# Gated cross-attention and mixture of experts on one core: another way to turn two batches, another gate layout, and a written order for loads and list fills

## The chip, the core and the metric

The kernel runs on one core of a Trainium2 chip. The metric is device time in microseconds (us) for one execution; the time of a kernel is the median of its runs. A core has five engines that run their own instruction streams and meet at semaphores: TensorE (PE; its weight loads are listed as PEld), VectorE (DVE), ScalarE (ACT), GpSimd (POOL) and SyncE (SP), which here mainly issues DMAs. Everything is computed in float32. Matrix products go to PSUM, a small memory from which DVE or ACT must copy the result before the buffer can be used again.

## The reference, cut to what matters

Four batches of 512 rows, 512 columns. Each batch goes through a cross-attention with 64 context rows and 16 heads, then through a mixture of 8 experts with the best 2 per row, plus one shared expert:

```python
x = x + tanh(g_xattn[0]) * xattn(layernorm(x), ctx, Wq, Wkv_expand, Wout)
x = x + tanh(g_ffn[0]) * ffn(layernorm(x), gate_w, w1, w2, w3, ws1, ws2, ws3)
...
# xattn: q = xn @ Wq.T; scores = q k / sqrt(32), causal mask, softmax, @ v, @ Wout.T
# ffn:
scores = softmax(xf @ gate_w.T)                 # 2048 x 8
weights, idx = top_k(scores, 2)
g = silu(xf @ w1[e].T) * (xf @ w3[e].T)
y = sum over the chosen e of weight * (g @ w2[e].T)
z = silu(xf @ ws1.T) * (xf @ ws3.T) @ ws2.T      # shared expert
```

## The kernel before, in words

**Tiling.** A batch is four token tiles of 128 rows (`QT = 4`), and 512 columns are four chunks of 128 (`DC = 4`). A product over 512 columns needs its input turned, columns on the partitions. Two normalised forms of every batch are turned: the first rows (input of the query projection, tile `xt`) and the second rows (input of the feed-forward part, tiles `x2t`). `turn` (L500) does it on PE: four 128x128 transposes for each token tile go to one PSUM buffer, and ACT copies that to SBUF (`transpose_rows`, L194).

**Attention loop (L693 to L795).** It runs over b = 0 to 3. In turn b PE does the scores of batch b, the first turn of batch b+1 (`turn(xn, xt)`, L701), the output projection of batch b-1 (`project_out`, L367, one 512-wide product for each token tile, product `pd`), the other half of the scores, the query projection of batch b+1 in four chunks (`project_q`, product `pq`), the turning of the probabilities (`transpose_p`, L340, product `pp`), the second turn and the gate of batch b-1, and the attention product (`po`). DVE meanwhile does masks, maxima, differences and sums of the softmax in four parts p0 to p3 (`largest`, `exponentials`, `softmax`), adds the projection to x (L374), takes moments (L156) and normalises (L185). ACT does exponentials and copies PSUM to SBUF. POOL divides by the sums (L338).

The order on PE, POOL, DVE and ACT is the order of the program text (`manual_schedule`, L844); what SP issues was placed by a scheduler. The four PSUM buffers of the pool `ps_mm` go round in order of allocation, so a product waits until the buffer of the fourth one before it has been copied out.

**Gate (L378 to L396).** `gate` does, for each of four column chunks k, one product of 32 gate columns (8 of them used) with all 512 tokens, each into its own 32 partitions of one buffer. ACT copies the 128x512 result; `gate_sum` then adds the four parts with four products, whose stationary operand is a 128x128 block of the parts and whose moving operand is `part`, a 0/1 matrix of 128x8. The result, tokens on partitions, goes to `choose` (L408), which finds the two best experts, the weights and the running counts.

**Routing.** `route` (L451) makes each row's place in a list per expert in DRAM (`xg_d`); POOL writes the rows there with indirect DMAs (L474). After the last batch, `fill_ends` (L535) writes a tile of null rows behind each of the eight lists: for each a register is loaded from SBUF and a DMA issued, all on SP. `tile_table` (L545) makes the table of tiles.

**Expert stage (from L998).** PE goes through the tiles of the lists: `hidden` (L911), `turn_g`, `down` (L939). A tile's rows come by SP's DMAs (`fetch`, L876) and are turned by DVE (`turn`, L900, in 32x32 blocks: the rows were stored with their columns permuted, `normalize(..., turned=True)`, and the DMA puts every fourth part on its own 32 partitions). POOL adds the results to `y_d` by indirect DMA (L949). Between attention and experts PE does products of the shared expert (`shared_in_turn`, L629), placed between the steps of the last routing by `fill`. At the end the sums are read back, added and stored.

**Loads.** Shared-expert weights `sh13` use the memory of `wq_sb`, so their load (L599) waits for the last query projection. `w13_all` (L850) and `w2_all` (L857) are loaded for all experts, 1 MB and 0.5 MB each; `w2_all` needs memory that the pool `al` (weights `wo_sb` and the attention output `at`) gives back.

Of the kernel before, what the change touches and what calls it, by code (L numbers as in the profile page):

```python
# [13 lines left out]
F32 = mybir.dt.float32  # L14
I32 = mybir.dt.int32
AF = mybir.ActivationFunctionType
ALU = mybir.AluOpType
AX = mybir.AxisListType

P = 128  # L20
B, S, D = 4, 512, 512
SK, L = 64, 128
NH, HD = 16, 32
NE, FF = 8, 256
DC = D // P
QT = S // P
NT = B * QT
FC = FF // P
# [8 lines left out]
ROWS = NE * REGION + (MAXT - TOPK * B * S // P) * P  # L37
# [11 lines left out]
def gated_cross_attention_moe(  # L49
# [14 lines left out]
    nc = tc.nc  # L64
    const = ctx.enter_context(tc.tile_pool(name="const", bufs=1))
    small = ctx.enter_context(tc.tile_pool(name="small", bufs=2))
    ET = mybir.EngineType
# [29 lines left out]
    y_d = dram.tile([2 * (B * S + P), YH], F32, name="y_d")  # L97
    y_rows = y_d.rearrange("(r h) d -> r (h d)", h=2)
    xg_w = dram_disjoint_views(xg_d, TOPK * NT + NE)
    y_w = dram_disjoint_views(y_d, 2)  # L100

    ident = const.tile([P, P], F32, name="ident")
    make_identity(nc, ident)
    ones = const.tile([P, P], F32, name="ones")
    nc.gpsimd.memset(ones, 1.0)

    part = const.tile([P, NE], F32, name="part")
    nc.gpsimd.tensor_copy(part, ident[:, 0:NE])
    for c in range(1, DC):
        nc.gpsimd.tensor_tensor(part, part, ident[:, c * HD : c * HD + NE], ALU.add)  # L110

    before = const.tile([P, P], F32, name="before")
    nc.gpsimd.affine_select(
# [40 lines left out]
    def moments(b, mv, t):  # L154
        st = small.tile([P, 6], F32, tag="st", name="st")
        nc.vector.bn_stats(st, xs[b][:, t, :])  # L156
        nc.vector.bn_aggr(mv[:, t, :], st)
# [21 lines left out]
    def normalize(xn, b, t, mv, rstd, turned=False):  # L179

        src = xs[b][:, t, :]
        if turned:
            src = src.rearrange("p (c a i) -> p a c i", c=DC, a=DC)
            xn = xn.rearrange("p (a c i) -> p a c i", a=DC, c=DC)
        nc.vector.tensor_scalar(  # L185
            xn, src, mv[:, t, 0:1], rstd[:, t, :], ALU.subtract, ALU.mult
        )

    def second_rows(w, c):


        return w[:, c, :].rearrange("(a i) n -> i a n", a=DC)
# [15 lines left out]
    x2t = [rows_sb[:, 0 : DC * S].rearrange("p (c s) -> p c s", c=DC)] + x2t  # L208

    ending = ctx.enter_context(ExitStack())  # L210
    al = ending.enter_context(tc.tile_pool(name="al", bufs=1, side="right"))
    weights = ctx.enter_context(ExitStack())

    with ExitStack() as attn:
# [162 lines left out]

        def gate(b):  # L378

            pg = ps_mm.tile([P, S], F32, tag="mm", name="pg")  # L380
            for k in range(DC):
                nc.tensor.matmul(
                    pg[k * HD : (k + 1) * HD, :], gate_sb[:, k, :], x2t[b][:, k, :],
                    start=True, stop=True,
                )
            parts = xr.tile([P, S], F32, tag="gate", name="parts")
            nc.scalar.copy(parts, pg)
            return parts

        def gate_sum(parts):  # L390
            pl = ps_mm.tile([P, QT, NE], F32, tag="mm", name="pl")
            for t in range(QT):
                nc.tensor.matmul(
                    pl[:, t, :], parts[:, ts(t, P)], part, start=True, stop=True
                )
            return pl  # L396

        full = [P, QT, NE]

# [92 lines left out]

        def first_rows(b, rest):
            rest()
            xn = [a4.tile([P, D], F32, tag="xn", name="xn") for t in range(QT)]
            for t in range(QT):
                normalize(xn[t], b, t, mv1[b], rstd1[b])
            return xn

        def turn(xn, dst):  # L500
            for t in range(QT):
                transpose_rows(xn[t], t, dst)
# [32 lines left out]
        def fill_ends(n):  # L535

            end = const.tile([P, NE], I32, name="end")
            nc.vector.tensor_tensor(end, n[:, :, 0], region[:, 0, :], ALU.add)
            for e in range(NE):
                r = nc.sync.value_load(end[0:1, e : e + 1], min_val=0, max_val=ROWS - P)  # L540
                nc.sync.dma_start(
                    out=xg_w[TOPK * NT + e][ds(r, P), :], in_=zeros[:, 0, :]
                )

# [51 lines left out]


        sh13 = const.tile([P, 2, DC, FF], F32, tag="wq_sh", name="sh13")
        for c in range(DC):  # L599
            for w in range(2):  # L600
                nc.sync.dma_start(
                    out=sh13[ts(c, HD), w], in_=second_rows(w13[0, :, w], c)
                )

        def shared_half(b, f, w, ph=None):
            if ph is None:
# [35 lines left out]


        def attention():
            xn = [a4.tile([P, D], F32, tag="xn", name="xn") for t in range(QT)]
            nc.gpsimd.tensor_copy(ctx_sb[:, :, 1, :], ctx_sb[:, :, 0, :])
            small_one = small.tile([P, 1], F32, tag="one", name="one", bufs=1)

# [44 lines left out]
            for b in range(B):  # L693
# [4 lines left out]
                    places, scatter = route(last - 1, *chosen)  # L698
                if more:
                    xt, qt_next = new_xt(), new_qt()  # L700
                    turn(xn, xt)  # L701
                if not b:
                    project_values(1)
                p0 = exponentials(*largest(psc, 0))
# [15 lines left out]
                if b:  # L720
                    for t in range(1, QT):
                        project_out(last, at, t)
                        moments(last, mv, t)
                    rest = deviation(mv, rstd)
                    if more:
                        table_of(AF.Exp)
                else:
                    project_q(xt, qt_next, range(2))
                    first_rest = first_moments(b + 2)
                    table_of(AF.Exp)  # L730
# [26 lines left out]
                if b:  # L757
                    transpose_p(p0, prt, 0)
                    transpose_p(p1, prt, 1)
                    turn(xn2, x2t[last])  # L760
                if more:
                    project_q(xt, qt_next, range(2, 3))
                    if b + 2 < B:
                        if b:
                            first_rest = first_moments(b + 2)
                            table_of(AF.Exp)
                        xn = first_rows(b + 2, first_rest)
                    project_q(xt, qt_next, range(3, DC))
                    if b:
                        scored = gate(last)  # L770
                else:
                    p3 = exponentials(*p3)
                    softmax(p3)
                    gated, scored = shared_pair(*next(parts), lambda: gate(last))
                    gated()
                    scores = gate_sum(scored)
                transpose_p(p2, prt, 2)
                if not b:
                    project_values(2)
                elif more:  # L780
                    scores = gate_sum(scored)
                transpose_p(p3, prt, 3)
                if not b:
                    project_values(3)
# [18 lines left out]
        def last_routing(at, chosen, parts):  # L803
            ps_f = ending.enter_context(tc.tile_pool(name="ps_f", bufs=2, space=PSUM))
            filling = shared_in_turn(parts, ps_f)

            def fill(n):
                for _ in range(n):
                    next(filling)

            def scatter_all(places, scatter):
                places()
                for t in range(QT):
                    scatter(t)

            b = B - 1
            xn2 = addressed([rows_sb[:, ts(t, ROW)] for t in range(QT)], b)
            mv, rstd = new_stats()
            for t in range(QT):
                project_out(b, at, t)  # L820
                if not t:
                    scatter_all(*route(b - 1, *chosen))
                moments(b, mv, t)
            deviation(mv, rstd)()
            second_rows_of(xn2, b, mv, rstd)
            fill(5)
            turn(xn2, x2t[b])
            fill(1)
            scored = gate(b)
            fill(1)  # L830
            chosen = choose(b, gate_sum(scored))
            fill(6)
            places, scatter = route(b, xn2, *chosen)
            n = counted()
            places()
            fill_ends(n)
            for t in range(QT):
                scatter(t)
            table = tile_table(n)
            for _ in filling:  # L840
                pass
            return table

        with tc.manual_schedule(engines={ET.PE, ET.Pool, ET.DVE, ET.Activation}):  # L844
            attended_last = attention()

            wup = weights.enter_context(tc.tile_pool(name="wup", bufs=1, reuse_waits="tile"))
            w13_all = wup.tile([P, NE, 2, DC, FF], F32, name="w13_all")
            for e in range(NE):
                nc.sync.dma_start(out=w13_all[:, e], in_=w13[1 + e])  # L850
            row_of, expert_of, rank_of, more = last_routing(*attended_last)

    ending.close()
    wdn = weights.enter_context(tc.tile_pool(name="wdn", bufs=1, reuse_waits="tile"))
    w2_all = wdn.tile([P, NE, FC, D], F32, name="w2_all")
    for e in range(NE):
        nc.sync.dma_start(out=w2_all[:, e], in_=w2[1 + e])  # L857

    turned.close()
    fp = ctx.enter_context(tc.tile_pool(name="fp", bufs=6, side="right", reuse_waits="tile"))  # L860
    tp = ctx.enter_context(tc.tile_pool(name="tp", bufs=3, side="right", reuse_waits="tile"))
# [259 lines left out]
```

## Time and profile before

| | us |
|---|---|
| median of 3 runs | 466.2 (465.54 to 466.81) |
| the profiled execution | 468.26 |
| its span, first to last instruction | 466.5 |
| attention, from the first scores to the last attention product | about 28 to 188 |
| last routing and shared expert | about 188 to 244 |
| expert tiles | about 244 to 433 |
| sums read back and stored | about 433 to 466 |

The granted TensorE clock was 0.998. Busy time, by stretches of the span:

| stretch, us | PE | DVE | ACT | POOL |
|---|---|---|---|---|
| 58.00 to 75.20 | 17.20 | 13.31 | 6.33 | 4.73 |
| 75.20 to 87.60 | 12.40 | 11.73 | 7.56 | 1.20 |
| 100.50 to 118.70 | 18.20 | 16.23 | 6.96 | 4.95 |
| 118.70 to 131.20 | 12.50 | 11.80 | 7.63 | 9.90 |
| 258.00 to 433.00 | 174.53 | 65.48 | 24.26 | 101.75 |

A row of the chain of waits is: start, length, engine, product and line. A row of the timeline is: start, length, engine, line, operation, output and inputs, shapes, count, and in brackets how long the engine was idle before it and what released it. Matmuls in float32 appear as two records each, transposes as one.

### The profile page before, as it was taken

How to read it: one execution, taken by the hardware profiler on the slowest of the kernel's cores; microseconds unless marked ns; L12 is line 12 of the kernel's file. 1: busy time of each engine (PE TensorE's matmuls, PEld its weight loads, DVE VectorE, ACT ScalarE, POOL GpSimd, SP SyncE). 2: the span in 40 equal slices, each digit the busy share in tenths (PEclk: the TensorE clock that was granted, in tenths of full speed). 3: DMA queues.
4: the chain of work that ended last, by engine and by line, in shares of the span. 5: the costliest groups of instructions: out<-in, count | busy, mean ns of one | idle time of the engine just before them, and what ended most of it. 6: DMA issues, size and time to landing. Idle time of an engine off the chain costs nothing.

```text
span 466.5 us, 6220 instructions
## 1 busy us (share of the span) xinstructions
PE 452.7 (97%) x1718; PEld 233.2 (50%) x1718; DVE 253.2 (54%) x605; ACT 131.2 (28%) x245; POOL 178.7 (38%) x188
## 2 busy tenths in 40 slices
PE   8999999999999989999999999999999999999894
PEld 6775455664555554445444444444444444444342
DVE  4659788779927984557322443333443333432385
ACT  2347652773454265413011111111111111111000
POOL 3003312302740473241500555555565655565300
PEclk9999999999999999999999999999999999999999
DMA  8996000000413040899883777666656666544498
GB/s 264 320 332 229 0 1 0 1 1 1 160 39 80 15 170 2 313 415 379 333 245 85 150 130 118 101 107 99 100 90 96 97 112 99 79 48 48 56 382 331
DMA packets 55423, 65.66 MB, mean 141 GB/s; under 512 B 11728, under 2 KB 40144, under 8 KB 54224
## 3 DMA queue, kind: packets, MB, share of 16 engines
q1 hardware_dynamic: 42736, 47.57, 32.4%
q0 software_dynamic: 12352, 17.57, 20.9%
q8 instruction: 17, 0.28, 0.3%
q14 instruction: 30, 0.25, 0.2%
q10 hardware_dynamic: 288, 0.00, 0.0%
HBM read 34.84 MB, written 30.27 MB: 140 GB/s over the span
## 4 chain that ended last, share of the span: by engine, by line
PE 84%; DMA 7%; DVE 6%; ACT 1%; issue 1%; SPq 0%; DVEq 0%
PE ph L915 24%; PE pd L370 12%; PE py L942 11%; PE pq L292 11%; PE ph L635 6%; DMA y_d<-y,meta 5%; PE ph L609 5%; PE psc L306 3%; PE pt L198 3%; PE pp L345 2%; DVE yk L1046 2%; PE po L359 2%; PE early L609 1%; PE pg L934 1%; DVE yk L1065 1%; DMA yk<-y_d 1%
## 5 line engine op out<-in xcount | busy, mean ns | idle before, releaser
L949 POOL DMA_INDIRECT y_d<-y,meta x68 | 105.6, 1553 | 103.4 <-DVE y L946 58.4
L915 PE MATMUL ph<-w_all,xgt 128*128 x272 | 122.5, 593 | 0.1
L338 POOL TENSOR_TENSOR pr<-pr,rs 128x1024 f32<-128x1024 f32 x16 | 30.3, 1901 | 117.7 <-DVE rs L337 103.5
L915 PEld LDWEIGHTS ph<-w_all,xgt 128*128 128x128 f32 x272 | 49.0, 190 | 49.8 <-issue 49.7
L942 PE MATMUL py<-w_all,gt 128*128 x136 | 63.9, 592 | 0.0
L926 DVE SCALAR_TENSOR_TENSOR g<-sl,w,ph 128x256 f32<-128x256 f32 x34 | 16.3, 480 | 83.8 <-ACT sl L924 81.3
L292 PE MATMUL pq<-xt,wq_sb 128*128 128x512 f32 (+1 forms) x160 | 56.9, 511 | 1.6 <-ACT prt L348 0.9
L370 PE MATMUL pd<-wo_sb,at 128*128 128x512 f32 x128 | 56.1, 595 | 0.0
L924 ACT ACTIVATE sl<-ph 128x256 f32<-128x256 f32 x34 | 13.1, 385 | 109.0 <-PE ph L915 61.1
L292 PEld LDWEIGHTS pq<-xt,wq_sb 128*128 128x128 f32 x160 | 29.7, 190 | 25.5 <-issue 20.1
L942 PEld LDWEIGHTS py<-w_all,gt 128*128 128x128 f32 x136 | 25.8, 190 | 32.5 <-issue 32.5
L946 DVE COPY y<-py 128x512 f32<-128x512 f32 x34 | 23.5, 692 | 27.8 <-PE py L942 27.8
L370 PEld LDWEIGHTS pd<-wo_sb,at 128*128 128x128 f32 x128 | 23.9, 190 | 29.1 <-issue 27.5
L976 PE MATMUL pz<-sh,gs_sb 128*128 128x512 f32 (+1 forms) x68 | 28.1, 570 | 1.7 <-DVE y L946 1.2
L635 PE MATMUL ph<-x2t,sh 128*128 128x512 f32 x64 | 28.6, 597 | 0.0
L936 ACT COPY gt<-pg 128x256 f32<-128x256 f32 x34 | 12.7, 373 | 53.1 <-PE pg L934 53.1
L903 DVE STREAM_TRANSPOSE xgt<-xg 128x512 f32<-128x512 f32 x34 | 23.9, 703 | 3.0 <-DMA xg<-xg_d 3.0
L156 DVE BATCH_NORM_STATS2 st<-x 128x6 f32<-128x512 f32 x32 | 21.7, 679 | 5.0 <-DMA x<-in_x_dram 4.5
L976 PEld LDWEIGHTS pz<-sh,gs_sb 128*128 128x128 f32 x68 | 12.7, 190 | 16.8 <-issue 15.4
L330 ACT ACTIVATE pr<-pr 128x1024 f32<-128x1024 f32 x16 | 17.0, 1064 | 13.6 <-DVE pr L329 10.9
L335 DVE TENSOR_REDUCE sm<-pr 128x16 f32<-128x1024 f32 x16 | 19.1, 1194 | 2.2 <-ACT pr L330 2.2
L329 DVE TENSOR_TENSOR pr<-psc,mx 128x1024 f32<-128x1024 f32 x16 | 19.5, 1219 | 0.4
(168 smaller groups left out, 495.7 us busy)
## 6 DMA issues: line engine op xcount, KB each, us to landing
xg<-xg_d SPq DMA_DIRECT2D x144, 64.0 KB
w_all<-in_w_dram SPq DMA_DIRECT2D x8, 1024.0 KB
y_d<-gs_sb SPq DMA_DIRECT2D x1, 4352.0 KB
w_all<-in_w_dram SPq DMA_DIRECT2D x8, 512.0 KB
yk<-y_d SPq DMA_DIRECT2D x8, 512.0 KB
out_dram<-yk SPq DMA_DIRECT2D x15, 256.0 KB
x<-in_x_dram SPq DMA_DIRECT2D x3, 1024.0 KB
xg_d<-gs_sb SPq DMA_DIRECT2D x8, 264.0 KB
```

Source lines behind the costliest of these rows:

```text
L156: nc.vector.bn_stats(st, xs[b][:, t, :])
L292: nc.tensor.matmul(pq, wq_sb[:, k, ts(c, P)], xt[:, k, tokens], start=(k == 0), stop=(k == DC - 1),)
L338: nc.gpsimd.tensor_tensor(pr, pr, rs.broadcast_to([P, NH, SK]), ALU.mult)
L370: nc.tensor.matmul(pd, at[:, c, ts(t, P)], wo_sb[:, c, :], start=(c == 0), stop=(c == DC - 1),)
L609: nc.tensor.matmul(ph, sh13[:, w, k, ts(f, P)], x2t[b][:, k, :], start=(k == 0), stop=(k == DC - 1),)
L635: nc.tensor.matmul(ph[:, w, :], sh13[:, w, k, ts(f, P)], x2t[b][:, k, :], start=(k == 0), stop=(k == DC - 1),)
L903: nc.vector.transpose(xgt.rearrange("p c t k -> p t c k"), xg.rearrange("p t (c i) -> p t c i", c=DC))
L915: nc.tensor.matmul(ph, xgt[:, k, :], w13_all[:, ds(e, 1), :, k, :], start=(k == 0), stop=(k == DC - 1),)
L942: nc.tensor.matmul(py, gt[:, f, :], w2_all[:, ds(e, 1), f, :], start=(f == 0), stop=(f == FC - 1))
L946: nc.vector.tensor_copy(y, py)
L949: nc.gpsimd.indirect_dma_start(out=y_w[h], out_offset=IndirectOffsetOnAxis(ap=goes[j][:, h : h + 1].bitcast(I32), axis=0), in_=y[:, ts(h, ...
L976: nc.tensor.matmul(pz, gs[b][:, f, ts(t, P)], sh2[:, f, columns], start=(f == 0), stop=(f == FC - 1),)
```

## The change

Six things change.

1. The first rows of batches 2 and 3 are no longer turned on PE. Once normalised (with permuted columns) they are written to DRAM by four DMAs on SP and read back by four more, each to 32 partitions; DVE then turns them with four instructions (`turn_blocks`), placed after the second token tile's moments in turns b = 1 and 2. `turn(xn, xt)` stays for batch 1 alone (b = 0). The rows of a batch are one tile now, with one buffer that the rows read back share.
2. In turns 1 and 2 the second turn (`turn(xn2, x2t[last])`) comes after the third chunk of the query projection, not before it.
3. The gate puts a token tile, not a column chunk, in each group of 32 partitions: 16 products of 32 columns with 128 tokens, the four chunks added in PSUM. ACT copies 128x128, and one PE transpose takes the place of `gate_sum`. `part` and the four POOL instructions that made it are gone.
4. `fill_ends` issues every other list's register load and DMA on ACT's queue.
5. SP joins the engines in written order. The `sh13` load is written after batch 3's query projection.
6. The pool `al` is closed after the last output projection, and all eight `w2_all` loads are written there, ahead of `fill_ends`.

```diff
+    xn_d = {b: dram.tile([S, D], F32, name=f"xn_d{b}") for b in range(2, B)}
...
-    part = const.tile([P, NE], F32, name="part")
-    nc.gpsimd.tensor_copy(part, ident[:, 0:NE])
-    for c in range(1, DC):
-        nc.gpsimd.tensor_tensor(part, part, ident[:, c * HD : c * HD + NE], ALU.add)
...
-            pg = ps_mm.tile([P, S], F32, tag="mm", name="pg")
+            pg = ps_mm.tile([P, P], F32, tag="mm", name="pg")
             for k in range(DC):
-                nc.tensor.matmul(
-                    pg[k * HD : (k + 1) * HD, :], gate_sb[:, k, :], x2t[b][:, k, :],
-                    start=True, stop=True,
-                )
-            parts = xr.tile([P, S], F32, tag="gate", name="parts")
-            nc.scalar.copy(parts, pg)
-            return parts
-
-        def gate_sum(parts):
-            pl = ps_mm.tile([P, QT, NE], F32, tag="mm", name="pl")
-            for t in range(QT):
-                nc.tensor.matmul(
-                    pl[:, t, :], parts[:, ts(t, P)], part, start=True, stop=True
-                )
-            return pl
+                for t in range(QT):
+                    nc.tensor.matmul(
+                        pg[ts(t, HD), :], gate_sb[:, k, :], x2t[b][:, k, ts(t, P)],
+                        start=(k == 0), stop=(k == DC - 1),
+                    )
+            scores = xr.tile([P, P], F32, tag="gate", name="scores")
+            nc.scalar.copy(scores, pg)
+            return scores
+
+        def by_token(scores):
+            pl = ps_mm.tile([P, QT, HD], F32, tag="mm", name="pl")
+            nc.tensor.transpose(pl.rearrange("p t e -> p (t e)"), scores, ident)
+            return pl[:, :, 0:NE]
...
         def first_rows(b, rest):
             rest()
-            xn = [a4.tile([P, D], F32, tag="xn", name="xn") for t in range(QT)]
+            xn = new_xn()
             for t in range(QT):
-                normalize(xn[t], b, t, mv1[b], rstd1[b])
-            return xn
+                normalize(xn[t], b, t, mv1[b], rstd1[b], turned=b > 1)
+            return passed(xn, b) if b > 1 else xn
+
+        def new_xn():
+            xn = ab.tile([P, QT, D], F32, tag="xn", name="xn")
+            return [xn[:, t, :] for t in range(QT)]
+
+        def passed(xn, b):
+            for t in range(QT):
+                nc.sync.dma_start(out=xn_d[b][ts(t, P), :], in_=xn[t])
+            xg = ab.tile([P, QT, QT, P], F32, tag="xn", name="xg")
+            for a in range(DC):
+                nc.sync.dma_start(
+                    out=xg[ts(a, HD)].rearrange("k t tb n -> k (t tb) n"),
+                    in_=xn_d[b][:, ts(a, P)].rearrange("(t k) n -> k t n", k=HD),
+                )
+            return xg
+
+        def turn_blocks(xg, dst):
+            for t in range(QT):
+                nc.vector.transpose(
+                    dst[:, :, ts(t, P)].rearrange("p c (tb k) -> p tb c k", k=HD),
+                    xg[:, t].rearrange("p tb (c i) -> p tb c i", c=DC),
+                )
...
-                r = nc.sync.value_load(end[0:1, e : e + 1], min_val=0, max_val=ROWS - P)
-                nc.sync.dma_start(
+                queue = nc.scalar if e % 2 else nc.sync
+                r = queue.value_load(end[0:1, e : e + 1], min_val=0, max_val=ROWS - P)
+                queue.dma_start(
...
-                    turn(xn, xt)
+                    if not b:
+                        turn(xn, xt)
...
                     for t in range(1, QT):
                         project_out(last, at, t)
                         moments(last, mv, t)
+                        if more and t == 1:
+                            turn_blocks(xn, xt)
...
                     transpose_p(p1, prt, 1)
-                    turn(xn2, x2t[last])
+                    if not more:
+                        turn(xn2, x2t[last])
                 if more:
                     project_q(xt, qt_next, range(2, 3))
+                    if b:
+                        turn(xn2, x2t[last])
...
                     project_q(xt, qt_next, range(3, DC))
+                    if b == B - 2:
+                        load_shared()
...
+            outputs.close()
+            wdn = weights.enter_context(tc.tile_pool(name="wdn", bufs=1, reuse_waits="tile"))
+            w2_all = wdn.tile([P, NE, FC, D], F32, name="w2_all")
+            for e in range(NE):
+                nc.sync.dma_start(out=w2_all[:, e], in_=w2[1 + e])
             deviation(mv, rstd)()
...
-        with tc.manual_schedule(engines={ET.PE, ET.Pool, ET.DVE, ET.Activation}):
+        with tc.manual_schedule(engines={ET.PE, ET.Pool, ET.DVE, ET.Activation, ET.SP}):
...
-    wdn = weights.enter_context(tc.tile_pool(name="wdn", bufs=1, reuse_waits="tile"))
-    w2_all = wdn.tile([P, NE, FC, D], F32, name="w2_all")
-    for e in range(NE):
-        nc.sync.dma_start(out=w2_all[:, e], in_=w2[1 + e])
```

## The prediction, made before the changed kernel was run

> **What bounds the kernel now.** I read the page first, then the chain of waits, then the timelines of DVE and ACT around the stage that the turns are taken from. On the page the reader is to see that PE is nearly all of the span, and what one DVE transpose costs, in a place where its rows have also come back from DRAM.
>
> ```profile
> PE 452.7 (97%) x1718; PEld 233.2 (50%) x1718; DVE 253.2 (54%) x605; ACT 131.2 (28%) x245; POOL 178.7 (38%) x188
> L903 DVE STREAM_TRANSPOSE xgt<-xg 128x512 f32<-128x512 f32 x34 | 23.9, 703 | 3.0 <-DMA xg<-xg_d 3.0
> ```
>
> From 185.77 to 432.5 us PE has no gap worth naming, and the tail behind its last tile hangs on that tile. So what PE gains or loses up to about 185 us the end gains or loses, if nothing new stalls behind it. The chain of waits (start, length, engine, product, line) in turn b = 1 shows what PE does there:
>
> ```profile
> 59.62 1.90 PE pt L198 x16
> 61.52 13.73 PE pd L370 x32
> 75.25 1.99 PE psc L306 x32
> 77.24 7.06 PE pq L292 x16
> 84.30 1.75 PE pp L345 x16
> 86.05 1.75 PE pt L198 x16
> 87.80 6.87 PE pq L292 x16
> 94.67 1.00 PE pg L382 x8
> 95.66 1.02 PE pp L345 x8
> 96.69 0.79 PE pl L393 x8
> 97.48 0.50 PE pp L345 x4
> ...
> 98.01 0.60 ACT prt L348
> ```
>
> The change removes the `pt` row at 59.62 (and its twin of 1.80 us in b = 2), shortens `pl`, and splits `pg`. All of it stands on the chain; the question is what else is nearly as late. DVE's timeline (the bracket is its idle time and the releaser) shows the spare time in which the new transposes must lie, first b = 1, then b = 2:
>
> ```profile
> 71.86 0.75 DVE L374 SCALAR_TENSOR_TENSOR x<-pd,tg_x,x 128x512 f32<-128x512 f32 x1
> 75.29 0.75 DVE L374 SCALAR_TENSOR_TENSOR x<-pd,tg_x,x 128x512 f32<-128x512 f32 x1 [1.74 <-PE pd L370]
> 77.29 1.23 DVE L324 TENSOR_REDUCE mx<-psc 128x16 f32<-128x1024 f32 x1
> 81.69 1.22 DVE L329 TENSOR_TENSOR pr<-psc,mx 128x1024 f32<-128x1024 f32 x1
> ...
> 116.63 0.72 DVE L374 SCALAR_TENSOR_TENSOR x<-pd,tg_x,x 128x512 f32<-128x512 f32 x1
> 118.82 0.75 DVE L374 SCALAR_TENSOR_TENSOR x<-pd,tg_x,x 128x512 f32<-128x512 f32 x1 [0.52 <-PE pd L370]
> ```
>
> ACT's timeline shows that behind DVE's last score difference (81.69) ACT has only 0.56 and 0.27 us free before the copies on which PE's third query chunk depends:
>
> ```profile
> 83.01 1.06 ACT L330 ACTIVATE pr<-pr 128x1024 f32<-128x1024 f32 x1 [0.56 <-DVE pr L329]
> 84.34 0.59 ACT L296 COPY qt<-pq 128x512 f32<-128x512 f32 x1 [0.27 <-PE pq L292]
> 84.83 1.57 ACT L348 COPY prt<-pp 128x512 f32<-128x512 f32 x3
> ```
>
> **The turns.** At face value PE loses 1.90 + 1.80 = 3.70 us (ACT loses eight copies too). DVE gains four transposes per turn. One after another, large DVE instructions there follow at about 0.09 us less than their length, so I take 0.62 us a step, 2.47 us in all (bound above: 4 x 0.703 = 2.81). They stand ahead of the third token tile's residual, where the row 71.86 is. In b = 1, PE's `pd` tiles come 1.90 us earlier, but DVE reaches the third tile at 71.86 + 2.47 = 74.33, the fourth at 75.9 (steps of 1.52 to 1.58 us, from the same instructions in b = 3), and the score maximum at 77.63 instead of 77.29: the idle 1.74 us has been eaten and 0.34 more. The last score difference then ends at 83.25, ACT's exponential starts at 83.35, its copy of query chunk 1 at 84.32 (0.97 us a step) and the first copy of turned weights runs 84.81 to 85.40. PE would have ended query chunk 1 at 82.40, but the last group of `pp` needs that chunk copied, and chunk 2 takes the PSUM buffer that the first `pp` copy frees (a ring of four): it starts at about 85.45. From there chunk 2, the second turn and chunk 3 are 3.43 + 1.75 + 3.43 = 8.61, so the gate starts at 94.06 where it stood at 94.67. Of the 1.90 us only 0.61 arrives. In b = 2 DVE had only 0.52 us free, so the same sum is worse: entering 1.19 us early (0.61 and the first gate), DVE reaches the score maximum 0.46 us later than before and the gate starts only 0.34 us earlier. PE came in 1.19 early; so this turn loses 0.85. Both turns together: -0.61 + 0.85 = +0.24 us, that is, nothing of the 3.70. Bounds: -3.70 if ACT and DVE do not hold PE, +0.9 with the longer step in both turns.
>
> **Rows by way of DRAM.** Batch 2's rows are normalised by 55.38 and wanted at 71.9: 16.5 us for 1 MB out and 1 MB back. Fast bound: the peak slice of 415 GB/s, 2 x 2.5 us. Slow bound: the last store of expert rows to its use took 5.46 us, and loads of rows in the expert stage at 92 GB/s would take 11.4: 16.9 together, 0.4 us late. Nearly nothing else moves there (0 to 1 GB/s in the page's slices) and SP's queue is idle, so I take 0. Batch 3's rows have 96.3 to 115.5: more. SP's later `sh13` loads stand behind a wait for a query chunk either way: 0. What would cost: landing after 71.9, since the waiting transpose holds the residuals behind it, and they hold `x`, the maxima and so ACT's exponentials.
>
> **The second turn**, moved behind chunk 2, is the same work: 0. Chunk 2 (3.43 us) now covers the normalising of its rows. `part`'s four POOL instructions (0.18 to 0.19 us) lay ahead of a wait for a DMA: 0.
>
> **The gate.** Per batch, `pl` goes from eight records (0.79) to one transpose, 0.11 by the `pp` rows (1.75 / 16): -0.68. `pg` goes from 8 records of 512 columns to 32 of 128, still over four column groups. Lower bound: eight records per group at 107 ns (a `pq` record of 512 columns takes 430 ns, a quarter is 107), 0.86. Upper bound: `psc`, also 32 records of 128 columns but only two row groups wide, 1.99. `psc` keeps each group busy 124 ns a record, eight of which are 0.99; with starting I take 1.1, nearest to the row of today's gate, 1.00, whose streamed columns per group are the same. Net -0.68 + 0.10 = -0.58 per batch, -2.32 for four; ACT's copy is 128 wide rather than 512, cheaper, and the wait for the weight copy at 98.01 stays as short. In b = 3 PE waited 1.37 us at 172.16 for such a copy; I leave that as it is. Each tenth in the gate's length is 0.4 us in the sum; the break-even lies at 1.62.
>
> Against that stands one more row and one rule. The weight loads of `po` start 16 within 0.18 us, so the sequencer is not slow there. The Trainium skill, "TensorE: Matmul & The Clock Gate", section "Back-to-back issue gap", says that with hardware decoding off each small matmul costs about 62 ns to issue; 32 of them would be 1.98 us (an estimate from that page), and the sum +1.4 instead of -2.1. No row here shows such a limit by itself. Another rule speaks against moving the turn: "VectorE: DVE Perf Modes", section "Rules for kernel authors", sends a 128x128 transpose to TensorE. The rows agree in price, 109 ns a block on PE against 703 / 4 = 176 on DVE; it is whose time is scarce that decides.
>
> **The expert stage.** `fill_ends` took SP 12.29 us for eight fills, 1.54 each. Four on ACT hold its queue about 6.1 us from 219.25 to 225.4, or to 228.7 if ACT's register load is as much slower as its row elsewhere (0.68 against 0.44 us). Behind them wait ACT's silu (0.60) and DVE's product (0.69) of the shared part, whose PSUM buffer PE wants at 227.25: 225.4 gives 226.7, in time; 228.7 gives 230.0, 2.8 us late. I take 0, by SP's row of the same instruction. The `w2` loads all going out ahead frees the first expert gather from traffic, and it is needed sooner: the first transposed rows were ready 0.34 us before PE wanted them. I take 0, with up to 1.7 us lost if the gather is no earlier.
>
> **Sum.** 0.24 - 2.32 = -2.1 us, against the profiled 468.26 (span 466.5 and 1.8 around it). The three times had a median of 466.2; the difference is applied to that: 464.1. About 1.4 us, 0.3%, is what a measurement of this kernel tells from no change.
>
> **The rivals.**
> 1. The turns come off whole: PE is held by nothing, -3.70 - 2.32 = -6.0, 460.2. For: DVE is 54% busy and waits for `pd`. Against: the 0.27 us of ACT above. Chance 0.09.
> 2. The small products of the gate do not overlap as today's do. At `psc`'s 1.99 the gate costs 4 x (0.99 - 0.68) = +1.24, and with 0.24 the sum is +1.5: 467.7, slower; one after another (32 x 107 ns = 3.4) +7. It decides from 1.62 us on. For: `psc`. Against: `psc` has two groups, the gate four. Chance 0.16.
> 3. The rows come back late. Each microsecond after 71.9 is one on DVE, so on PE; 2.5 late in each turn gives +2.9, 469.1. It decides from about 1.1 us in each. For: the read back takes pieces of 128 elements, 512 bytes, in a rearranged order. Against: idle DMA engines. Chance 0.10.
> 4. ACT's fills hold the silu: up to +2.8, 464 to 467. Chance 0.07.
>
> **How the numbers follow.** The forecast has 0.58: mostly faster (0.43), some same (0.13), as a gate of 1.3 would bring it within 1.4 us of before. With rival 1 and a part of 4, faster is 0.54; same 0.20; slower 0.26. The range runs from 461.3 (half the turns' gain) to 468.2 (gate at `psc`'s rate, and some lateness); outside are rival 1 whole, a serial gate and rows more than 2 us late, under 2 in 10. The forecast's own range is 463 to 465.5.
>
> **What would show it.** PE waits in b = 1 and 2 ahead of query chunk 2, ended by ACT's `prt` or `qt` copy; four DVE transposes of 0.70 with no idle time by a DMA; `pg` at 1.0 to 1.2 us and `pl` at 0.11; no PE wait for ACT's L640 silu or for `xgt`; the tail as long as before. It is wrong if `pg` is near 2, if the transposes wait for `xg`, or if PE's `pd` to `pq` run without a gap.

## The result and the profile after

| | us |
|---|---|
| before, median of 20 runs | 466.16 (465.17 to 467.89) |
| changed, median of 20 runs | 465.13 (463.39 to 466.65) |
| ratio | 0.9974, 95% interval 0.9961 to 0.9986 |
| profiled run of the changed kernel | 463.80 (span 462.1), clock 0.998 |

The change gains a quarter of a per cent where 2.1 us, 0.45%, was forecast; two later comparisons (experiment 5) find less, 0.5 and 0.3 us, and can't tell that from nothing. The profiled run stands 4.5 us under that of before (468.26), which no pair of medians shows: 2.9 us of it belong to the first profile of before alone, as experiment 1 shows.

The chain of waits of the changed kernel in turn b = 1 (start, length, engine, product, line):

```profile
56.12 2.01 PE psc L304 x32
58.16 1.24 DVE psc L321
...
70.27 2.49 DVE xt L517 x4
73.43 0.70 DVE st L153
76.20 1.28 ACT L162
78.71 1.14 DVE pr L327
79.84 1.14 DVE mx L322
81.01 1.24 DVE pr L327
82.39 0.90 issue
84.57 3.53 PE pq L290 x8
88.10 1.75 PE pt L195 x16
89.85 3.44 PE pq L290 x8
93.28 1.01 PE pg L382 x32
```

Before, this stretch was PE's alone. Now the chain runs through DVE from 58 us on, over the four transposes (2.49 us) and through a row of ACT (76.20, a table load) back to PE at the third query chunk. PE's timeline shows what that makes of PE, first in b = 1, then in b = 2 (in brackets the idle time before the row and its releaser):

```profile
83.91 0.66 PE L343 MATMUL pp<-ident,pr 128*128 128x128 f32 x4 [1.51 <-ACT qt L294]
84.41 3.69 PE L290 MATMUL pq<-xt,wq_sb 128*128 128x512 f32 x8
...
93.21 1.08 PE L382 MATMUL pg<-rows_sb,gate_sb 128*32 128x128 f32 x32
94.22 1.09 PE L343 MATMUL pp<-ident,pr 128*128 128x128 f32 x8
95.15 0.27 PE L392 MATMUL pl<-ident,scores 128*128 128x128 f32 x1
...
127.64 0.66 PE L343 MATMUL pp<-ident,pr 128*128 128x128 f32 x4 [2.07 <-ACT qt L294]
128.13 3.69 PE L290 MATMUL pq<-xt,wq_sb 128*128 128x512 f32 x8
```

Two waits have taken the place of the two removed turns: 1.51 and 2.07 us, both for ACT's copy of query chunk 1 (a third, of 0.29 us in b = 2, is for the last DVE transpose). The gate's 32 small records start to `pp` in 1.01 us and its one transpose takes 0.11 from start to start. One thing in ACT's timeline has changed that no edit names:

```profile
76.20 1.28 ACT L162 ACT_TABLE_LOAD   x1 [10.76 <-DVE ve L160]
77.50 0.20 ACT L162 ACTIVATE sd<-ve 128x4 f32<-128x4 f32 x1
...
108.51 1.28 ACT L162 ACT_TABLE_LOAD   x1
120.47 0.20 ACT L162 ACTIVATE sd<-ve 128x4 f32<-128x4 f32 x1 [10.67 <-DVE ve L160]
```

The same rows in ACT's timeline of before, in b = 1:

```profile
66.98 1.28 ACT L165 ACT_TABLE_LOAD   x1
77.23 0.21 ACT L165 ACTIVATE sd<-ve 128x4 f32<-128x4 f32 x1 [8.96 <-DVE ve L163]
```

In b = 1 the table of the square root is now loaded after the variances (`ve`) are there. Before, it was loaded at 66.98, ten microseconds ahead of the root at 77.23, while ACT had nothing to do. Now DVE waits 0.48 us for the root (DVE's row of line 166 at 77.73). Apart from the copies of turned rows, which are gone, the order of ACT's instructions is the same. Why the load waits for the variances is not shown: the missing copies alone can't be the reason, since they are missing in b = 2 too, and there the load is early (108.51).

### The profile page after: what moved, and what is told of

It is laid out like the page before. It is cut to its first block, busy times and chain, and to the rows that moved or that the text cites. A ratio compares the mean times of both kernels' runs of the same rounds, so it can differ in the third digit from the quotient of the medians.

```text
span 462.1 us, 6310 instructions
## 1 busy us (share of the span) xinstructions
PE 445.0 (96%) x1754; PEld 228.0 (49%) x1754; DVE 257.3 (56%) x613; ACT 125.1 (27%) x237; POOL 178.5 (39%) x184
## 4 chain that ended last, share of the span: by engine, by line
PE 77%; DVE 17%; ACT 3%; issue 2%; DMA 1%; DVEq 0%; ACTq 0%
PE ph L947 25%; PE py L974 13%; PE pq L290 8%; PE pd L368 6%; PE ph L659 6%; PE ph L633 5%; PE pz L1008 3%; DVE pr L327 3%; DVE mx L322 2%; DVE st L153 2%; PE pt L195 2%; PE psc L304 2%; DVE yk L1078 2%; PE pg L966 2%; PE po L357 2%
## 5 line engine op out<-in xcount | busy, mean ns | idle before, releaser
L343 PE MATMUL pp<-ident,pr 128*128 128x128 f32 x128 | 16.4, 275 | 3.6 <-ACT qt L294 3.6
```

## The experiments

Three groups were run, each on one chip of its own, beside runs of before: 465.05 in the first (experiments 1 to 4), 466.58 in the second (5, 6, 7 and 9) and 464.77 in the third (5, 8 and 9). Experiment 10 is one profile by itself. Differences are to the before of the same group.

**1. Before, again.**

> The kernel before, unchanged. In its first profile the eight key-projection records at the start took 3.75 us, in the changed kernel 1.97 for the same eight, and everything behind them was 1.5 us later. Theory A: this differs from run to run and has nothing to do with the change; here the median is 466.2 again, and if the records take 1.97 us in this profile its span is about 465.0. Rival B: it belongs to the kernel before (its four POOL instructions more at the start, say); then the records take 3.75 us again and the span is 466.5.

Measured 465.11 against 465.05. PE's timelines at the start and at b = 3, first those of the first profile of before, then of this one:

```profile
6.93 3.75 PE L270 MATMUL pk<-ctx_sb,wkv_sb 128*128 128x256 f32 x8 [0.60 <-DMA wkv_sb<-in_wkv_dram]
...
173.53 1.14 PE L198 MATMUL pt<-ident,xn 128*128 128x128 f32 x8 [1.37 <-ACT prt L348]
```

```profile
6.81 2.29 PE L270 MATMUL pk<-ctx_sb,wkv_sb 128*128 128x256 f32 x8 [0.48 <-DMA wkv_sb<-in_wkv_dram]
...
169.84 1.91 PE L198 MATMUL pt<-ident,xn 128*128 128x128 f32 x16
```

Theory A: the slow key projection did not come again, nor did the wait of 1.37 us. The span is 463.6, 2.9 us less: the gate of b = 1 stands 1.3 us earlier, and the turning at b = 3 takes 1.6 us less. Rival B falls for good with the last profile of experiment 5, where the changed kernel needs 3.75 us for the same eight records. So from here on the traces are compared with this one. The wait at b = 3 (0.8 to 1.4 us, behind a late ACT copy) stands in 7 of the 14 profiles, of before and of changed kernels alike; why ACT is late there was not found.

**2. The new gate alone.**

```diff
# before.py, with nothing of the change but gate, by_token and the removal of part
```

> Before, with the new gate alone (no gather part, one transpose, 16 small products); the turns, fills and loads as before. Theory A: in the traces each gate shortened PE's line by 0.66 to 0.73 us, so -2.8 us in all, about 463.4. Rival B: part of the gate's gain is taken back by the wait for ACT's copy of the turned weights, and only 1.2 us, the whole of what the change measured, comes from it: 465.0.

Measured 462.73, 2.3 us below before, ratio 0.9939 (0.9918 to 0.996), all ten mean clocks 0.996 or more. The traces give 0.7 us for each gate, 2.8 in all; the median gives 2.3 and the ratio 2.8. The gate alone gains more than the whole change (1.0 in its own comparison), so the rest of the change loses some 1.3 us or more.

**3. The changed kernel with the old gate.**

```diff
-            pg = ps_mm.tile([P, P], F32, tag="mm", name="pg")
+            pg = ps_mm.tile([P, S], F32, tag="mm", name="pg")
...
-                    scores = by_token(scored)
+                    scores = gate_sum(scored)
```

> The changed kernel with the old gate (gather part and the four POOL instructions that make it back), all else as changed. Theory A: the turns lose 1.1 us by DVE and ACT, the other edits change nothing or win up to 1.0 (a shorter wait in b = 3 and the tail): 466.2 to 467.3, and PE still waits 1.5 and 2.1 us ahead of the third query chunk. Rival B: the turns are worth their 3.7 us and something else in the change lost them: 463 or less.

Measured 471.75, 6.7 us above before (ratio 1.0132, 1.0092 to 1.0171): neither theory. Its trace shows two things that were not reckoned with. Behind the wait of b = 2 the third query chunk took 5.39 us for the same eight records, at a granted clock of 0.73 from 128 to 132 us. And ahead of the first expert tile that runs only if the lists are long enough, PE waited for nothing that the profile shows, with half the clock after it (0.50 from 420 to 424 us):

```profile
420.88 6.62 PE L953 MATMUL ph<-w_all,xgt 128*128 x8 [3.11 <-issue]
```

Less these (1.7 + 3.1 + 3.0 of 473.4 in that run) it is at 465.6, 0.6 us below the low end of theory A.

**4. The square root's table loaded early.**

```diff
                 p1 = exponentials(*largest(psc, 1))
+                if b == 1:
+                    table_of(AF.Sqrt)
```

> The changed kernel with one square root of a one on ACT behind the exponentials of turn b = 1, so that the table of the square root is loaded while ACT is idle (it was loaded 1.28 us behind the variances, at 76.20, and DVE waited 0.48 us for the root). Theory A: DVE and ACT set PE's pace there, so the gate of b = 1 starts 0.5 us earlier and the end comes 0.5 us earlier (more, up to 0.8, if ACT's query copy gets ahead of the exponential): about 464.6 if the changed kernel is 465.1. Rival B: the 0.48 us lies in slack: no difference.

Measured 463.16, 1.9 us below before (ratio 0.9958, 0.9938 to 0.9977), where the changed kernel's three ratios are 0.9974 and, below, 0.9989 and 0.9985. ACT's and PE's timelines:

```profile
65.53 1.28 ACT L675 ACT_TABLE_LOAD   x1
66.83 0.20 ACT L675 ACTIVATE one<-ones 128x1 f32<-128x1 f32 x1
76.24 0.20 ACT L162 ACTIVATE sd<-ve 128x4 f32<-128x4 f32 x1 [9.21 <-DVE ve L160]
```

```profile
83.41 0.66 PE L343 MATMUL pp<-ident,pr 128*128 128x128 f32 x4 [0.94 <-ACT qt L294]
```

The load is back in ACT's idle time, PE's wait shrinks from 1.51 to 0.94 us, and measured from the end of batch 0's work the gate stands 0.56 us earlier. Theory A, by the trace. The median is another matter: it lies 0.9 to 1.6 us further below before than the changed kernel's three medians do. The changed kernel did not run in this group, and the intervals overlap. Only 3 of the 12 runs have a mean clock of 0.995 or less, where the changed kernel has 24 of 44 (experiment 5); whether the shorter wait is the reason is not shown.

**5. The changed kernel beside before, twice.**

> The changed kernel, unchanged, beside before on one chip. Theory A (the granted clock): its two new PE waits of 1.5 and 2.1 us ahead of the third query chunk are in some runs followed by some 3.4 us at half the clock, 1.7 us each time, as the trace with the old gate showed at 128 us. Then the times fall in steps, the runs with a mean clock of 0.992 to 0.995 being 1.5 to 3 us above those with 0.997 to 0.999, and the median is 1 to 1.5 us below before though the trace of a run at the full clock is about 1.5 to 2 below. Rival B: the spread is a matter of the first runs' chip; then the runs agree within 1 us.

> The changed kernel once more, beside the next two on one chip. Theory A (a PE wait of about 2 us is in many runs followed by half the clock): some runs with a mean clock of 0.995 or less, these 1.5 us or more above the others; median 0.5 to 1.5 us below before. Rival B: all runs within 1 us.

Measured 466.04 against 466.58 (ratio 0.9989, 0.9969 to 1.0009) and 464.52 against 464.77 (0.9985, 0.9965 to 1.0006). The last one, sorted, with the mean granted clock of each run:

```
462.43 0.998   462.62 1.000   462.70 0.996   463.00 0.999   463.70 0.999   464.01 0.998
465.04 0.995   465.29 0.992   465.44 0.992   465.60 0.994   466.00 0.994   467.39 0.992
```

Theory A's steps are there: in the last one every run at 0.995 or less is over 1 us above all the others; in the first the two kinds overlap by 0.1 us. The medians, 0.5 and 0.3 us below before, fall short of the 1 to 1.5 and 0.5 to 1.5 expected. Rival B falls: the runs spread over 4.5 and 5.0 us. The clock is not the whole spread, since the runs of before lie up to 3.3 us apart in the first of these groups, with no mean clock under 0.996.

Both profiles show where the clock goes. PE's timeline of the first, and its windows (stretch, length, busy time of PE, PEld, DVE, ACT and POOL with counts, granted clock, DMA share, GB/s):

```profile
127.69 0.66 PE L343 MATMUL pp<-ident,pr 128*128 128x128 f32 x4 [2.07 <-ACT qt L294]
128.18 5.39 PE L290 MATMUL pq<-xt,wq_sb 128*128 128x512 f32 x8
```

```profile
120.00:128.00 8.00, 5.93 (x26) 3.25 (x25) 7.76 (x17) 5.12 (x8) 6.58 (x15) 1.00 0.52 203
128.00:132.00 4.00, 4.00 (x10) 1.76 (x8) 2.55 (x4) 1.58 (x4) 2.67 (x3) 0.63 0.00 0
132.00:136.00 4.00, 4.00 (x22) 2.62 (x21) 0.00 (x0) 2.39 (x5) 1.25 (x1) 0.95 0.00 0
```

The wait is the same 2.07 us as in the first profile of the changed kernel, but there the eight records behind it took 3.69 us and here 5.39: PE has fallen to half its clock for some 3.4 us, and 1.7 us are lost. (In slices of 0.5 us the clock column reads 0.50 from 129.0 to 132.0. The two windows add up to the same: 4 x (1 - 0.63) + 4 x (1 - 0.95) = 1.68 us lost, at half the clock 3.4 us.) In the second profile the wait is 2.08 us and the chunk takes 5.39 us again; its start is 1.6 us late besides, by the slow key projection of experiment 1.

A run that was not profiled has only its mean clock. It can be read as a sign, because the 14 profiles agree: the five with a mean of 0.995 or less all have a stretch at half the clock ahead of the tail, the nine with 0.996 or more have none. (In the tail, where PE has ended, all 14 have one.) Of the 44 timed runs of the changed kernel (the 20 of the first comparison and these 24) 24 have a mean clock of 0.995 or less, and lie 0.3 us above before (median of the differences); the other 20 lie 1.9 us below. Of the 79 runs of before with a clock on record none is under 0.996.

**6. Both turns back on PE.**

```diff
-                normalize(xn[t], b, t, mv1[b], rstd1[b], turned=b > 1)
-            return passed(xn, b) if b > 1 else xn
+                normalize(xn[t], b, t, mv1[b], rstd1[b], turned=False)
+            return xn
...
-                    if not b:
-                        turn(xn, xt)
+                    turn(xn, xt)
...
-                        if more and t == 1:
-                            turn_blocks(xn, xt)
```

> The changed kernel, but the first rows of batches 2 and 3 are turned by PE as before, without the way through DRAM (the second turn stays behind the third query chunk); gate, fills, loads and SP's order as changed. Theory A: the turns on DVE cost more than they bring (trace: the gate of b = 1 +0.1, of b = 2 +0.9, and the clock's part), and the other edits are worth nothing: the time is that of the new gate alone, 2.3 us below before, no mean clock under 0.996. Rival B: the fills, the loads and SP's order bring or cost something too: then it differs from 2.3 below by over 1 us.

Measured 464.10, 2.5 us below before (ratio 0.996, 0.9946 to 0.9974), no clock under 0.996: theory A, the gate alone. The list fills on ACT, the `w2` loads ahead, SP's order and the moved second turn are together worth nothing that can be measured (one by one they were not run), and the way through DRAM with its transposes loses what the changed kernel lacks, 1.9 us in this group.

**7. A longer wait.**

```diff
                             turn_blocks(xn, xt)
+                            turn_blocks(xn, xt, range(2))
```

> The changed kernel with the first two of the four transposes done twice in turns b = 1 and 2 (the same values again), 1.24 us more on DVE in each, so that PE's two waits grow to about 2.7 and 3.3 us. Theory A (DVE sets the pace, and a longer wait makes the clock fall nearly always): 2.5 us for the work and up to 3.4 for two stretches at half the clock, 4 to 6 us above the changed kernel, with mean clocks of 0.989 to 0.994. Rival B (DVE sets the pace, the clock has nothing to do with PE's waits): 2.5 us above, clocks as before. Rival C (DVE has slack there): under 1 us above.

Measured 470.03, 4.0 us above the changed kernel of the same group; mean clocks 0.990 to 0.995 in all six runs. The gate of b = 1 moves by 1.2 us, as DVE's two transposes more would have it. In b = 2 the longer wait came in two pieces, 1.48 us for the last transpose and 2.12 us for the copy of chunk 1, not as one of 3.3; behind the second the third chunk takes 5.39 us. Theory A, at the low end of its range, as far as six runs can tell: all six show the low mean clock, where the changed kernel of the same group shows it in 8 of 12. Behind the wait of b = 1, now 2.65 us, the clock stayed up in this profile.

**8. The same wait, filled.**

```diff
+                def busy():
+                    for _ in range(6):
+                        nc.tensor.matmul(
+                            psc[:, 0, 0, 0].rearrange("p j k -> p (j k)"), ident, ident,
+                            start=True, stop=True,
+                        )
...
-                    transpose_p(p1, prt, 1)
+                    transpose_p(p1, prt, 1, *([busy] if more else []))
```

> The changed kernel, with six products of the identity by itself put on PE inside its two new waits (between the third and fourth group of the turned weights in b = 1 and 2, 12 records, 1.3 us of the 1.5 and 2.1 us; they write a score buffer that is already read, and nothing reads them). They add work and take no wait away. Theory A (it is the clock that makes the changed kernel slower than its own trace): PE stays busy, the clock stays up, no run has a mean clock under 0.996, and the median is 1 to 1.5 us below that of the changed kernel. Rival B (the spread has another cause): the same as the changed kernel or up to 0.3 us above.

Measured 462.68, 1.8 us below the changed kernel of the same group (464.52), and 2.1 below before (ratio 0.9962, 0.9947 to 0.9976); one mean clock of twelve is at 0.995, none lower. PE's timeline in b = 2:

```profile
126.28 1.60 PE L788 MATMUL psc<-ident 128*128 128x128 f32 x12 [0.45 <-DVE pr L327]
127.90 0.66 PE L345 MATMUL pp<-ident,pr 128*128 128x128 f32 x4
128.40 3.69 PE L290 MATMUL pq<-xt,wq_sb 128*128 128x512 f32 x8
```

The twelve useless records lie where PE waited. The third chunk starts no earlier for them, 29.73 us behind the first scores of the turn where it was 29.71 in the first profile of the changed kernel, and yet the kernel is quicker. That is theory A, but for the one run at 0.995: a sum of work and waits has no term that adding work would make smaller. The six runs of the changed kernel in this group whose clock stayed up have a median of 462.85, and the filled kernel comes out there.

**9. Three tiles of batch 2 and one of batch 3 by DVE, the rest by PE.** It was run in two groups.

```diff
+        by_dve = [0, 0, 3, 1]
...
-                normalize(xn[t], b, t, mv1[b], rstd1[b], turned=b > 1)
+                normalize(xn[t], b, t, mv1[b], rstd1[b], turned=t < by_dve[b])
...
-                    if not b:
-                        turn(xn, xt)
+                    turn(xn, xt, by_dve[b + 1])
...
-                            turn_blocks(xn, xt)
+                            turn_blocks(xg, xt, by_dve[b + 1])
```

> The changed kernel, but DVE turns only three of the four tiles of batch 2 and one of batch 3, and PE the rest. Worked out from the trace of before: ahead of the third query chunk PE had 0.94 us more to do than DVE and ACT, so a turned tile moved off PE (0.475 us) gains until DVE's 0.62 us a tile has used that up: three tiles in b = 1, one in b = 2. Theory A: -1.2 us in b = 1 and -0.45 in b = 2, against the same kernel with the turns on PE, and no waits long enough for the clock: some 3.5 to 4 us below before, the best so far. Rival B: DVE has no room at all there; then it is no better than with the turns on PE, 2.3 below before.

> Three tiles of batch 2 and one of batch 3 turned by DVE, again, for its interval. Theory A: 4 to 4.5 us below before (ratio 0.990 to 0.992), all mean clocks at 0.996 or above since PE does not wait in b = 1 and 2. Rival B: the four runs before were lucky; under 3 us below.

Measured 462.17 against 466.58 (ratio 0.9905, 0.989 to 0.9921) and 460.69 against 464.77 (0.9906, 0.9885 to 0.9927): 4.1 to 4.4 us below before, the best of all kernels run here: theory A both times, in the first group by 0.4 us more than it said. PE's timeline of the second, in b = 1 and in b = 2:

```profile
81.77 2.08 PE L343 MATMUL pp<-ident,pr 128*128 128x128 f32 x16
83.69 3.69 PE L290 MATMUL pq<-xt,wq_sb 128*128 128x512 f32 x8
...
124.35 1.91 PE L343 MATMUL pp<-ident,pr 128*128 128x128 f32 x16
126.10 3.60 PE L290 MATMUL pq<-xt,wq_sb 128*128 128x512 f32 x8
```

All four groups of `pp` are in one row, without a wait of their own (in b = 1 they take 2.08 us, 0.17 more than in experiment 6), and no mean clock is under 0.996. Against the trace of experiment 6 the gates stand 1.0 us earlier in b = 1 and 0.5 more in b = 2, where 1.2 and 0.45 were worked out. One PE turn stays in b = 1, its copy on ACT too, and ACT's table load is early again by itself (65.92). Other splits were not run, so whether three and one is the best is not known.

**10. The old gate once more, one profile.**

> The changed kernel with the old gate, one more profile. The first one had, besides half the clock behind the wait of b = 2, a PE wait of 3.1 us at 417.8 us that nothing in the profile releases, ahead of the first expert tile that only runs if there are enough lists, and half the clock behind it too. Theory A: the wait belongs to this program: it is there again, of 2 to 4 us. Rival B: it was chance: here PE waits under 0.5 us there, as in the other kernels, and the span is about 3 to 6 us shorter.

```profile
420.71 5.20 PE L953 MATMUL ph<-w_all,xgt 128*128 x8 [3.52 <-issue]
```

The wait is there again, with half the clock behind it: in two profiles of two it belongs to that program, and none of the other 12 profiles has it. What in it makes PE wait for nothing visible is open; it is not in the changed kernel, whose wait at this place is 0.2 us.

## Why the prediction was right, and what it had not seen

The time lay inside the range and the sign was right; of the 2.1 us about half arrived in the median of the first comparison, and about a quarter and an eighth in the two later ones. The mechanism was right for the turns and the gate; that the sum of the trace, -1.73, comes so near to -2.08 is partly luck, since 0.82 us lost on the turns stand against 0.47 more won on the gates. Step by step, against the trace of experiment 1, each stretch counted from the last one:

| step | forecast | trace of the changed kernel |
|---|---|---|
| turn of b = 1, up to the gate | -0.61 | +0.13 |
| turn of b = 2, up to the gate | +0.85 | +0.93 |
| four gates | -2.32 | -0.72, -0.73, -0.68, -0.66 = -2.79 |
| sum | -2.08 | -1.73 |
| clock behind the waits | not seen | 0 here, 1.7 in the two other profiles |

The rows run from the first scores of a turn to its gate (b = 1: 56.05 to 93.21, in experiment 1 56.29 to 93.32). They are not the whole span: the turn of b = 3 took 1.13 us longer in this profile, by the wait behind a late ACT copy that comes and goes, and the spans differ by 1.5 us.

- *The turns give nothing.* Right, and for the reason given: DVE and ACT take over the pace, and rival 1 falls. They lose 1.06 us in the trace where 0.24 was forecast. DVE's steps came out as summed (2.49 for 2.47 us; the third tile 2.42 us behind the place where its row was). The term for b = 1 was 0.74 us too good. 0.56 of it is the table load, as experiment 4 shows: the forecast took the load as it stood in before, in ACT's idle time. Why it moved in b = 1 alone is open, and so are the other 0.18.
- *The gate.* The mechanism was right; its length was 1.01 where 1.1 was taken, and the rest came with the `pl` term. Rival 2 falls: 32 records start within 1.01 us, 32 ns each. The Trainium skill's 62 ns for each small matmul with hardware decoding off ("TensorE: Matmul & The Clock Gate", section "Back-to-back issue gap") does not show here; whether decoding was on or off, no run tells.
- *Rows by way of DRAM.* Right: the rows that left from 52.5 us on were back by about 64, by the DMA share of the windows (0.70 from 62 to 64 us, 0.02 in the next two), and DVE wanted them at 70.27; no transpose waits for a DMA. Rival 3 falls.
- *Fills, `w2`, SP's order, the moved second turn.* Right at 0: ACT's fills take 5.0 us and its silu stands at 221.52, PE has no wait there, and experiments 2 and 6 gain the same, 2.3 and 2.5 us. Rival 4 falls.
- *What failed* is the line "In b = 2 DVE had only 0.52 us free, so the same sum is worse": it priced PE's new wait by its length alone. In two of the three profiles of the changed kernel the wait of 2.07 us is followed by half the clock, which costs 1.7 us, nearly as much again; by the mean clocks it is so in 24 of 44 runs. That took the median from about 1.9 us below before, where the runs at the full clock are, to 0.3 to 1.0 below. No rival named it. The Trainium skill has the mechanism, with a limit of some 3.4 us of idle time (the same page, section "HAM oscillation — how this bites in real kernels"); here a wait of 2.07 to 2.12 us in b = 2 was followed by it in four of seven profiles, one of 1.5 us in b = 1 in none of five, and one of 2.65 us not in the one profile that has it. What decides between the runs is not shown.
- *The range.* Its lower end, 461.3, is not what its label says: the gates' 2.32 and half of the turns' 3.70 make 462.0. Nothing hangs on it here.

So the change is two changes: a gate that gains 2.3 to 2.8 us, and a move of work from PE to DVE that loses 0.1 us in one place and 0.9 in the other, and in over half of the runs the clock besides. Cut down to three tiles and one, the same move gains another 1.7 to 1.9 us on top of the gate by the medians, 1.5 by the traces.

## What to carry to other kernels

When work is moved off the busiest engine, work out how far the next chain lies behind it, and move just that much. Here a tile saved PE 0.475 us and cost DVE 0.62, and DVE had 1.74 us idle in b = 1 and 0.52 in b = 2: room for 2.8 tiles and for 0.8 (an estimate from these rows of before). Three and one gained, four and four lost. A wait that is made on PE has a second price where the granted clock can fall; read the clock of the windows behind each new wait and of every timed run, not of one profile, and where a wait of 2 us can't be avoided, try putting work into it: here that gained 1.8 us. Look at the spread before explaining a difference of two single profiles: of the 4.5 us between the first two, 2.9 had nothing to do with the change.

## What was not expected of the hardware

- Twelve matmul records that nothing reads made the kernel 1.8 us quicker (464.52 to 462.68).
- A PE wait of 2.07 us was followed by about 3.4 us at half the granted clock in two of the three profiles of the changed kernel, and 24 of its 44 runs have the low mean clock that goes with it.
- The same eight key-projection records took 3.75 us in one profile of before and one of the changed kernel, 2.29 in another of before and 1.97 in most others, with a granted clock of 1.00 on record in all of them.
- A PE wait of 3.1 to 3.5 us at the first conditional expert tile, with no releaser on record, in both profiles of one program and in no other.
